# Cross-attention on one core: keys and values of each batch from 15 block products over three thirds of the keys in place of 18 products over two halves

## Chip, cores and metric

The kernel runs on one core of a Trainium2 chip. The metric is the device time of one execution in microseconds. Three executions of the kernel before gave a median of 989.63 us (988.45 to 991.03). A further execution was profiled; it took 991.36 us, and the span that its profile covers, from the first to the last instruction, is 989.6 us. All numbers are fp32.

## What is computed

There are 16 batches. Each has 100 query rows of 640 numbers (x) and 722 context rows of 384, of which 718 are keys and values of an ordinary attention with 8 heads of 80, and the last 4 are tokens of a second, small attention. The result is projected, and the input is added. Cut to what matters:

```python
enc, ca = ctx[:, :718], ctx[:, 718:]
query, keyt, valt = x @ Wq, enc @ Wk, enc @ Wv
hs = mha(query, keyt, valt)                    # 8 heads, softmax over 718 keys
ca_q1 = einsum('btc,th->bch', ca, Wq_ca)[:, indices, :]
ca_hs1 = mha(ca_q1, x, x)                      # 100 rows, keys and values are x
ca_hs2 = mha(ca_hs1 @ Wq, ca @ Wk_ca, ca @ Wv_ca)   # 4 keys
out = (hs + ca_hs2) @ Wout + b_out + x
```

For this case three products matter most: keyt and valt (718 x 384 by 384 x 640 for each batch), and what they feed, the scores and the weighted sum of the values.

## The kernel before

The engines are TensorE (PE, matmuls into PSUM), VectorE (DVE) and ScalarE (ACT), which read PSUM, GpSimd (POOL), which works in SBUF alone, and SyncE (SP), from whose queue most DMAs are issued. [...]

The kernel runs over the batches b in one unrolled loop. A turn of the loop makes the scores of batch b, then its values and the keys of batch b + 1, then the weighted sum of batch b. In more detail:

- *Scores* (`scores`, matmuls at L507). s_ps = K^T Q for 718 keys in three pairs of blocks; ACT copies them to SBUF (st, L517). DVE takes the maximum over keys (L1022, L1041), and the class `Maximum` turns it over the partitions in steps: turned (transpose), quad, side and mx (reductions), spread (ACT copies), over (a transpose on DVE, L581). Then DVE subtracts `over` from st (L1007, three instructions of 1,600 columns), and ACT takes the exponential of each (L1017).
- *Values and keys* (`Blocks`, matmuls at L304). The keys are cut into two halves of 359, the first 256 of the 384 input columns into two chunks, and the weights' columns into two halves. A fast 2 x 2 scheme makes the product of the first two chunks from 7 block products in place of 8, and the third chunk adds 4: 11 matmuls of one block of rows. Values have three blocks of rows (128, 128 and 103 keys of each half), each with `first_half` and `second_half` over four PSUM banks, 33 matmuls of 320 columns. Keys have the first four of their five row chunks in two such groups, and the fifth, `last_keys` (L448), is made from 6 plain matmuls: 28 matmuls of 359 columns. A product's bank is read at each step, by an ACT copy where a result block begins and by a DVE add to what is already there otherwise.
- *Sums of inputs.* The scheme needs sums of blocks of the context. `enc_sums` makes them on POOL, four instructions of 359 columns for each batch (L352), one batch ahead. Those of the weights are made once, in batch 0, on POOL (`weight_sums`, L365). In batch 0 the values and keys are plain products (`first_values`, L279, and `first_keys`), and of these values the last six matmul groups come inside the loop's first turn.
- *Weighted sum.* a_ps (L1147), 96 matmuls of 81 columns, the 81st being the sum of the weights.
- *The small attention* (class `Second`): y_ps (L613), the scores on POOL (`scores1`, L648 and L655, ten or so instructions of 800 columns), z_ps (L676), `values2` on POOL (L738 and L745), the load vb (L695). `keys(b)` multiplies m, which the start computes for all batches, by a mask into m2 on POOL.
- *Output.* Rows are collected to chunks of 128 over the batches; hst_ps and o_ps (L816) come in some batches only, and the queries of two batches (q_ps, L422) in every second one.

From batch 0 on, PE, DVE and POOL run in the order in which the code stands (`tc.manual_schedule`); ACT's order was left to a scheduler, with `issue_after` in some places. SP and the DMA queues are ordered by the scheduler as well. [...]

PSUM is cut into two pools of four banks, ps4 and ps1. The context of a batch (enc, with three more columns of 359 for the sums) has two buffers, so that batch b + 2 is loaded when batch b's values are done.

Of the kernel before, what the change touches and what calls it, by code (L numbers as in the profile page):

```python
# [8 lines left out]
F32 = mybir.dt.float32  # L9
# [9 lines left out]
P = 128  # L19
HC = H // P  # L20
CC = CAD // P
KH = SK // 2

KC = [(u + k, P) for u in (0, KH) for k in (0, P)] + [(u + 2 * P, KH - 2 * P) for u in (0, KH)]
NP = len(KC) // 2

PAIR = [(0, 0), (1, 0), (0, 1), (1, 1), (2, 0), (2, 1)]
PC = [KC[PAIR.index((i, 0))] for i in range(NP)]
# [59 lines left out]
S1, S2, S4 = range(3)  # L88
T1, T2, T4 = range(3)
# [3 lines left out]
def kernel(  # L93
# [28 lines left out]
    ps4 = ctx.enter_context(tc.tile_pool(name="ps4", bufs=4, space=PSUM))  # L122
    ps1 = ctx.enter_context(tc.tile_pool(name="ps1", bufs=4, space=PSUM))

    def psum4(name, n=4):
        return [
            ps4.tile([P, 512], F32, tag="ps4", name=f"{name}_{j}") for j in range(n)
        ]

    def four1(name):  # L130
        return [psum1(f"{name}_{j}") for j in range(4)]
# [3 lines left out]


    def wide(name):
        return main.tile([P, ROWS], F32, tag="wide", name=name, bufs=3)
# [7 lines left out]
    def hsT_tile(name):  # L146
        return main.tile([P, HC, P], F32, tag="hsT", name=name, bufs=3)

    def xn_tile(name):
        return main.tile([P, H], F32, tag="xn", name=name, bufs=3)  # L150
# [12 lines left out]
    def enc_tile(name):  # L163

        enc = inp.tile([P, CC * SK + 3 * KH], F32, tag="enc", name=name)
        return (
            enc[:, : CC * SK].rearrange("p (c k) -> p c k", c=CC),
            enc[:, CC * SK :].rearrange("p (j k) -> p j k", j=3),
        )

    def load_enc(b):
        enc = enc_tile(f"enc_{b}")
        nc.sync.dma_start(out=enc[0], in_=enct[b])
        return enc

# [3 lines left out]
    wv_sb = const.tile([P, CC, H], F32, name="wv_sb")  # L179
    wq_sb = const.tile([P, HC, H], F32, name="wq_sb")  # L180
    wk_sb = const.tile([P, CC, H], F32, name="wk_sb")
    kT = const.tile([P, HC, SK], F32, name="kT")
    wout_sb = const.tile([P, HC, H], F32, name="wout_sb")
    bias = const.tile([P, H], F32, name="bias")


    wv2 = const.tile([P, 3, H // 2], F32, name="wv2")
    wk2 = const.tile([P, 3, 2, P], F32, name="wk2")
    wk4 = const.tile([P, P], F32, name="wk4")

    wvca_sb = enc_tile("wvca")[0][:, :, :H]
    enc = enc_tile("enc_0")
    for c in range(CC):
        in_order(nc.sync.dma_start(out=enc[0][:, c, :P], in_=enct[0][:, c, :P]))
    for cols in slice(0, H // 2), slice(H // 2, H):
        for c in range(CC):
            nc.scalar.dma_start(
                out=wv_sb[:, c, cols], in_=wv[c * P : (c + 1) * P, cols]
            )
    for lo, hi in [(P, KH), (KH, SK)]:  # L200
        in_order(nc.sync.dma_start(out=enc[0][:, :, lo:hi], in_=enct[0][:, :, lo:hi]))
# [5 lines left out]
    wqt_sb = wout_sb  # L207
    in_order(nc.sync.dma_start(out=wqt_sb, in_=wqt.rearrange("(c p) r -> p c r", p=P)))
    xT = inp.tile([P, 2, HC, S], F32, tag="xT", name="xT_0")
    in_order(nc.sync.dma_start(out=xT, in_=xt[0:2].rearrange("b p c s -> p b c s")))  # L210
    for c in range(HC):
        in_order(nc.sync.dma_start(out=kT[:, c, :CAD], in_=packed(wkt, c)))  # L212
# [10 lines left out]
    vs = []  # L223
    for i in range(NP):
        v = const.tile([PC[i][1], 4, NH // 2, D + 1], F32, name=f"v_{i}")
        nc.gpsimd.memset(v[:, :, :, D : D + 1], 1.0)
        vs.append(v)

    def block(i, g):

        i, u = PAIR[i]
        return vs[i][:, 2 * u + g]
# [27 lines left out]
    m = const.tile([P, HC, B, HT], F32, name="m")  # L260
# [11 lines left out]
    def first_values(i, enc, engines, halves=(0, 1)):  # L272

        k, n = KC[i]
        for g in halves:
            engine = engines[g]
            v_ps = psum1(f"v_ps_0_{i}_{g}")
            for c in range(CC):
                nc.tensor.matmul(  # L279
                    v_ps[:n, : H // 2],  # L280
                    enc[0][:, c, k : k + n],
                    wv_sb[:, c, g * (H // 2) : (g + 1) * (H // 2)],
                    start=(c == 0),
                    stop=(c == CC - 1),
                )
            engine(
                block(i, g)[:, :, :D],
                v_ps[:n, : H // 2].rearrange("p (h d) -> p h d", d=D),
            )


    class Blocks:
        def __init__(self, name, a, w, to, view, swap):


            self.name, self.a, self.w, self.to, self.view = name, a, w, to, view
            self.swap = swap

        def sum(self, j, *products, first=False, last=False):
            bank = self.banks[j]  # L300
            for i, (a, w) in enumerate(products):
                a, w = self.a[a], self.w[w]
                left, right = (w, a) if self.swap else (a, w)
                nc.tensor.matmul(  # L304
                    bank[: left.shape[1], : right.shape[1]],
                    left,
                    right,
                    start=(first and i == 0),
                    stop=(last and i == len(products) - 1),
                    skip_group_check=True,  # L310
                )
            return self.view(bank)

        def first_half(self, room=None):

            self.banks = room or four1(f"{self.name}_ps")
            c11, c12, c21, c22 = self.to
            m = self.sum(0, ("11", "11"), first=True)
            self.copies = [nc.scalar.copy(c22, m)]
            m = self.sum(1, ("S2", "T2"), first=True)  # L320
            nc.vector.tensor_tensor(c21, m, c22, ALU.add)  # L321
            m = self.sum(2, ("S1", "T1"), first=True)
            nc.vector.tensor_tensor(c22, m, c22, ALU.add)
            m = self.sum(3, ("S3", "T3"), first=True)
            nc.vector.tensor_tensor(c22, m, c22, ALU.add)

        def second_half(self, behind=None, ahead=None):

            if ahead:
                ahead()  # L330
                behind = behind()
            c11, c12, c21, c22 = self.to
            m = self.sum(0, ("12", "21"), ("31", "31"), last=True)
            with tc.issue_after(behind.ins) if behind else nullcontext():
                self.copies.append(nc.scalar.copy(c11, m))
            m = self.sum(1, ("32", "32"), last=True)
            nc.vector.tensor_tensor(c22, m, c22, ALU.add)
            m = self.sum(2, ("S4", "22"), ("31", "32"), last=True)
            nc.vector.tensor_tensor(c12, m, c21, ALU.add)
            m = self.sum(3, ("22", "T4"), ("32", "31"), last=True)  # L340
            nc.vector.tensor_tensor(c21, m, c21, ALU.add)

    def sums(to, raw):

        (a11, a12), (a21, a22) = raw
        for out, left, right, op in (
            (to[S1], a21, a22, ALU.add),
            (to[S2], to[S1], a11, ALU.subtract),
            (a21, a11, a21, ALU.subtract),
            (to[S4], a12, to[S2], ALU.subtract),  # L350
# [3 lines left out]
    def weight_sums(to, raw, steps=range(4)):  # L354

        (w11, w12), (w21, w22) = raw
        all_steps = (
            (to[T1], w12, w11, ALU.subtract),
            (to[T2], w22, to[T1], ALU.subtract),
            (to[T4], w21, to[T2], ALU.subtract),  # L360
            (w12, w22, w12, ALU.subtract),
        )
        for i in steps:
            out, left, right, op = all_steps[i]
            nc.gpsimd.tensor_tensor(out, left, right, op)  # L365

    def enc_sums(enc):
        raw, to = enc
        sums(
            [to[:, j] for j in range(3)],  # L370
            [[raw[:, c, u * KH : (u + 1) * KH] for c in range(2)] for u in range(2)],
        )

    def a_blocks(enc, k, n):
        raw, to = enc
        half = lambda c, u: raw[:, c, u * KH + k : u * KH + k + n]
        blocks = {j: to[:, i, k : k + n] for j, i in (("S1", S1), ("S2", S2), ("S4", S4))}
        blocks |= {"11": half(0, 0), "12": half(1, 0), "S3": half(0, 1), "22": half(1, 1)}
        return blocks | {"31": half(2, 0), "32": half(2, 1)}

    def w_blocks(raw, to):
        blocks = {"T1": to(T1), "T2": to(T2), "T3": raw(0, 1), "T4": to(T4)}
        return blocks | {
            f"{c + 1}{u + 1}": raw(c, u) for c in range(CC) for u in range(2)
        }

    wv_blocks = w_blocks(
        lambda c, u: wv_sb[:, c, u * (H // 2) : (u + 1) * (H // 2)],
        lambda j: wv2[:, j],
    )  # L390
    wk_blocks = [
        w_blocks(
# [833 lines left out]
```

## Time and profile before

Busy time of the engines in some stretches of the profiled execution, in microseconds. The loop's turn for a batch begins with its scores.

| stretch | length | PE | DVE | ACT | POOL |
|---|---|---|---|---|---|
| whole span | 989.6 | 978.3 | 666.2 | 313.5 | 487.0 |
| first keys and queries, 43.1 to 61.2 | 18.10 | 18.10 | 6.92 | 4.02 | 9.55 |
| batch 0, 61.2 to 104.3 | 43.10 | 41.58 | 33.06 | 17.54 | 33.57 |
| batch 1, 104.3 to 165.4 | 61.10 | 59.85 | 43.23 | 21.03 | 34.37 |
| batch 2, 165.4 to 222.1 | 56.70 | 56.70 | 41.60 | 18.36 | 29.85 |
| batch 3, 222.1 to 287.0 | 64.90 | 64.90 | 41.60 | 20.20 | 29.86 |

How to read the rows of the profile: a row of the timeline has start, busy time, engine, line, operation, what it writes and reads (by the program's names; out<-in), sizes, and how many instructions were put together (xN). A bracket at the end has the idle time of the engine before the row and what ended it. A row of the groups has the busy time of all instructions of one kind and the mean of one in nanoseconds, then the idle time before them. Names are those of buffers, so a bank that was first used as `room` keeps that name. The chain of waits follows the work that ended last back through what released it.

### The profile page before, as it was taken

How to read it: one execution, taken by the hardware profiler on the slowest of the kernel's cores; microseconds unless marked ns; L12 is line 12 of the kernel's file. 1: busy time of each engine (PE TensorE's matmuls, PEld its weight loads, DVE VectorE, ACT ScalarE, POOL GpSimd, SP SyncE). 2: the span in 40 equal slices, each digit the busy share in tenths (PEclk: the TensorE clock that was granted, in tenths of full speed). 3: DMA queues.
4: the chain of work that ended last, by engine and by line, in shares of the span. 5: the costliest groups of instructions: out<-in, count | busy, mean ns of one | idle time of the engine just before them, and what ended most of it. 6: DMA issues, size and time to landing. Idle time of an engine off the chain costs nothing.

```text
span 989.6 us, 25057 instructions
## 1 busy us (share of the span) xinstructions
PE 978.3 (99%) x10945; PEld 746.6 (75%) x10945; DVE 666.2 (67%) x1227; ACT 313.5 (32%) x600; POOL 487.0 (49%) x440
## 2 busy tenths in 40 slices
PE   9999999999999999999999999999999999999998
PEld 6686869677696777868678686786868768697776
DVE  1249893967739677486955769468674776838784
ACT  1234342414333143332422333133331423314241
POOL 4557762665605646172652726536372562714604
PEclk9999999999999999999999999999999999999999
DMA  8642111120302202011120111201111030210101
GB/s 280 195 142 72 44 51 44 42 100 8 113 3 67 75 8 87 24 57 66 52 69 24 65 58 52 69 23 58 38 64 57 8 107 3 68 48 1 44 2 34
DMA packets 18533, 59.93 MB, mean 61 GB/s; under 512 B 2232, under 2 KB 9208, under 8 KB 14904
## 3 DMA queue, kind: packets, MB, share of 16 engines
q1 hardware_dynamic: 14888, 40.46, 12.5%
q0 software_dynamic: 2512, 16.72, 5.4%
q8 instruction: 86, 1.41, 0.6%
q10 hardware_dynamic: 1024, 1.15, 0.4%
q14 instruction: 23, 0.19, 0.1%
HBM read 54.07 MB, written 4.26 MB: 59 GB/s over the span
## 4 chain that ended last, share of the span: by engine, by line
PE 95%; DMA 2%; SPq 1%; DVE 1%; issue 1%; ACT 0%; ACTq 0%; DVEq 0%
PE room L304 19%; PE v_ps L304 18%; PE s_ps L507 12%; PE a_ps L1147 11%; PE k_ps L304 10%; PE kT_ps L448 7%; PE q_ps L422 7%; PE o_ps L816 6%; PE y_ps L613 2%; DMA wq<-in_wq 1%; SPq L212 1%; PE z_ps L676 1%; PE hst_ps L789 1%; PE v_ps L279 1%; DMA wv_sb<-in_wv 0%
## 5 line engine op out<-in xcount | busy, mean ns | idle before, releaser
L648 POOL TENSOR_TENSOR e<-ca,g 100x800 f32<-100x800 f32 x64 | 99.2, 1561 | 320.3 <-PE v_ps L304 248.6
L738 POOL TENSOR_TENSOR hs<-vb,p 100x640 f32<-100x640 f32 x64 | 83.9, 1322 | 135.9 <-DVE st L1007 105.0
L304 PE MATMUL v_ps<-wv_sb,enc 128*128 128x320 f32 (+1 forms) x480 | 149.5, 434 | 0.6 <-DVE v L321 0.6
L517 ACT COPY st<-s_ps 128x400 f32<-128x400 f32 (+1 forms) x192 | 80.6, 505 | 125.2 <-PE s_ps L507 125.1
L304 PEld LDWEIGHTS v_ps<-wv_sb,enc 128*128 128x128 f32 (+1 forms) x480 | 84.7, 179 | 42.4 <-DVE v L321 1.1
L1147 PEld LDWEIGHTS a_ps<-v,st 128*64 128x64 f32 (+3 forms) x3072 | 109.0, 125 | 7.6 <-issue 7.5
L1147 PE MATMUL a_ps<-v,st 128*64 128x81 f32 (+3 forms) x3072 | 112.0, 233 | 1.2 <-issue 1.2
L1017 ACT ACTIVATE st<-st 128x1600 f32<-128x1600 f32 (+1 forms) x48 | 73.8, 1538 | 101.8 <-DVE st L1007 101.8
L1007 DVE TENSOR_TENSOR st<-st,over 128x1600 f32<-128x1600 f32 (+1 forms) x48 | 104.1, 2174 | 0.0
L507 PE MATMUL s_ps<-qp,kT 32*128 32x100 f32 (+1 forms) x3072 | 99.6, 265 | 1.2 <-issue 1.2
L507 PEld LDWEIGHTS s_ps<-qp,kT 32*128 32x128 f32 (+1 forms) x3072 | 96.4, 181 | 3.1 <-issue 1.7
L655 POOL TENSOR_TENSOR e<-e,e 100x800 f32<-100x800 f32 x48 | 90.3, 1882 | 3.8
L304 PE MATMUL room<-enc,wk_sb 128*128 128x359 f32 x240 | 82.3, 465 | 0.0
L304 PE MATMUL k_ps<-enc,wk_sb 128*128 128x359 f32 x240 | 82.2, 464 | 0.0
L1022 DVE TENSOR_TENSOR most<-most,st 128x800 f32<-128x800 f32 (+1 forms) x64 | 65.1, 1016 | 25.3 <-ACT st L517 24.2
L745 POOL TENSOR_TENSOR hs<-hs,hs 100x640 f32<-100x640 f32 x48 | 74.0, 1541 | 3.8
L304 PE MATMUL room<-wv_sb,enc 128*128 128x320 f32 x240 | 74.4, 432 | 0.0
L422 PEld LDWEIGHTS q_ps<-xT,wq_sb 128*128 128x128 f32 x400 | 67.9, 190 | 2.1 <-issue 0.5
L448 PE MATMUL kT_ps<-enc,wk_sb 128*128 128x359 f32 x210 | 68.5, 465 | 0.8 <-DVE wk_sb L920 0.8
L422 PE MATMUL q_ps<-xT,wq_sb 128*128 128x200 f32 x400 | 69.1, 333 | 0.0
L1158 DVE RECIPROCAL rs<-a_ps 100x4 f32<-100x4 f32 x32 | 5.8, 181 | 92.8 <-PE a_ps L1147 92.7
L816 PE MATMUL o_ps<-wout_sb,hsT 128*128 128x320 f32 x240 | 66.8, 433 | 0.0
(138 smaller groups left out, 1535.5 us busy)
## 6 DMA issues: line engine op xcount, KB each, us to landing
enc<-in_enct SPq DMA_DIRECT2D x15, 1077.0 KB
vb<-va_d POOLq DMA_DIRECT2D x16, 1000.0 KB, 6.5
xT<-in_xt SPq DMA_DIRECT2D x8, 500.0 KB
xn<-in_x SPq DMA_DIRECT2D x12, 320.0 KB
out<-xn SPq DMA_DIRECT2D x11, 320.0 KB
ca<-in_cas SPq DMA_DIRECT2D x16, 156.2 KB
wout_sb<-in_wqt SPq DMA_DIRECT2D x1, 1600.0 KB
wq<-in_wq SPq DMA_DIRECT2D x5, 320.0 KB
```

The costliest lines, as they stand in the source:

```text
L304: nc.tensor.matmul(bank[: left.shape[1], : right.shape[1]], left, right, start=(first and i == 0), stop=(last and i == len(products) - 1), ...
L422: nc.tensor.matmul(q_ps[:, : 2 * S].rearrange("p (j s) -> p j s", j=2), wq_sb[:, c, n * P : (n + 1) * P], xT[:, :, c, :], start=(c == 0), ...
L448: nc.tensor.matmul(k_ps[:, :KH], w, a, start=(c == 0), stop=(c == CC - 1))
L507: nc.tensor.matmul(s_ps[r][:n, 256 * a + lo : 256 * a + hi], kT[rows, c, k : k + n], rhs, start=(a == 0 and c == 0), stop=(c == HC - 1), s ...
L517: copied = nc.scalar.copy(st[:, :, 2 * r * S : 2 * (r + 1) * S], s_ps[r][:n].rearrange("p (a q) -> p a q", a=2)[:, :, : 2 * S],)
L648: first = nc.gpsimd.tensor_tensor(to, self.ca[:, t, :].unsqueeze(1).to_broadcast([S, NH, S]), g[:, :, t].unsqueeze(2).to_broadcast([S, NH, ...
L655: nc.gpsimd.tensor_tensor(e, e, to, ALU.add)
L738: first = nc.gpsimd.tensor_tensor(to, vb[:S, t, :].rearrange("p (h d) -> p h d", h=NH), p2[:, :, t].unsqueeze(2).to_broadcast([S, NH, D]), ...
L745: nc.gpsimd.tensor_tensor(sums, sums, to, ALU.add)
L816: nc.tensor.matmul(o_ps[k][:n, : H // 2], hsTs[r][:, c, :n], wout_sb[:, c, k * (H // 2) : (k + 1) * (H // 2)], start=(c == 0), stop=(c == ...
L1007: less = nc.vector.tensor_tensor(st[i], st[i], top.over[:n].unsqueeze(1).to_broadcast([n, 2, ROWS]), ALU.subtract,)
L1147: nc.tensor.matmul(a_v[lo:hi, h % 4], st[i // 2][:, i % 2, h * S + lo : h * S + hi], block(i, h // 4)[:, h % 4], start=(i == 0), stop=(i = ...
```

## The change

The keys are cut into three thirds of 240, each overlapping the next by one key (KT = 240; a third u begins at key 239 u), and the 384 input columns into three chunks. A 3 x 3 by 3 x 2 scheme makes the six result blocks (third u, half g of the weights' columns) from 15 block products in place of 18. Two tables give its order: `V_PLAN` for values, `K_PLAN` for keys, each entry a bank, a product number and the result block that the bank is read into. Products go on adding up in the same bank after it was read.

- `Values` does two matmuls of 120 x 320 for each product (two halves of the third), `Keys` two of 128 x 240 (two chunks of the keys' rows). The fifth chunk of the keys stays plain: nine matmuls of 240 columns. For a batch that is 30 matmuls of 320 columns for values (33 before), and 39 of 240 for keys (28 of 359 before).
- A bank's reading (`Blocks.go`) is an ACT copy where the result block begins, and a DVE add otherwise. Banks A and B of the values are pairs of banks, read by one instruction of 640 columns. A read of the keys has 480 columns.
- PSUM is cut anew: ps2 has two pairs, psk two banks (A and B of the keys), ps1 two banks, for C, D and E of both values and keys and for y_ps, z_ps and a_ps.
- Products of the values of batch b and of the keys of batch b + 1 take turns (`both`), and `top.go` stands between them.
- `enc_sums` has 13 instructions of 240 columns. Two of the nine raw blocks of a batch lie in a tile of their own, `rest`, with one buffer, loaded by `load_rest`; the sums overwrite others. `weight_sums` has 12 steps, for wk on DVE, for wv on POOL (seven early, five late).
- m goes to DRAM (m_d, five writes from ACT's queue), and each batch loads its part (mb) from SP's queue.
- ACT too runs in the order of the code. The exponentials stand directly behind their subtractions, the third one behind the copies of `last_keys`.
- The tile `most` is kept, wide tiles have two buffers for three, and so have hsT and xn. Copies of the scores are two of 800 columns for two of the three pairs. The last batch uses free room of enc.

The diff, cut to its core. The first `open` is that of `Values`, which opens A and B beforehand, as pairs; the second is that of `Keys`. The orders at the end are those of batch 0 (it begins at `second.scores1()`) and of batches 1 to 14 (`second.scores1(seen)`):

```diff
-    ps4 = ctx.enter_context(tc.tile_pool(name="ps4", bufs=4, space=PSUM))
-    ps1 = ctx.enter_context(tc.tile_pool(name="ps1", bufs=4, space=PSUM))
+    ps2 = ctx.enter_context(tc.tile_pool(name="ps2", bufs=2, space=PSUM))
+    psk = ctx.enter_context(tc.tile_pool(name="psk", bufs=2, space=PSUM))
+    ps1 = ctx.enter_context(tc.tile_pool(name="ps1", bufs=2, space=PSUM))
...
+V_PLAN = [
+    ("A", 7, (2, 1)),
+    ("B", 13, (1, 0)),
+    ("D", 1, (2, 0)),
+    ("A", 3, (2, 0)),
+    ("B", 8, (2, 0)),
+    ("E", 6, (1, 0)),
+    ("A", 9, (1, 0)),
+    ("B", 10, (2, 1)),
+    ("C", 12, (0, 1)),
+    ("A", 2, (0, 0)),
+    ("C", 11, (2, 1)),
+    ("B", 4, (0, 1)),
+    ("A", 0, (0, 1)),
+    ("B", 14, (0, 0)),
+    ("A", 5, (1, 1)),
+]
+K_PLAN = [V_PLAN[k] for k in (0, 1, 2, 3, 4, 5, 6, 7, 9, 11, 8, 12, 10, 13, 14)]
...
+    def rest_tile(name):
+        return main.tile([P, len(A_REST), KT], F32, tag="rest", name=name)
...
+    def load_rest(b, enc):
+        rest = rest_tile(f"rest_{b}")
+        for (u, c), i in A_REST.items():
+            nc.sync.dma_start(
+                out=rest[:, i], in_=enct[b][:, c, u * (KT - 1) : u * (KT - 1) + KT]
+            )
+        return enc[0], rest
...
+        def go(self, n=1):
+            for _, (k, (bank, f, to)) in zip(range(n), self.plan):
+                first = bank not in self.opened
+                if first:
+                    self.opened[bank] = self.open(bank)
+                at = self.opened[bank]
+                self.product(at, f, first, self.ends[bank] == k)
+                for out, left in self.places(at, to):
+                    if to in self.begun:
+                        self.moved = nc.vector.tensor_tensor(out, left, out, ALU.add)
+                    else:
+                        self.moved = nc.scalar.copy(out, left)
+                self.begun.add(to)
...
+        def open(self, bank):
+            return [psum1(f"v_ps{bank}_{self.b}_{j}") for j in range(2)], None
...
+        def open(self, bank):
+            return (psumk if bank in "AB" else psum1)(f"k_ps{bank}_{self.b}")
...
+        nc.scalar.dma_start(out=m_d[c], in_=m_sb[c])
...
+            second.scores1()
+            weight_sums(nc.gpsimd, wv_sb, True)
+            top.go(3)
+            kk.go(3)
...
+            second.scores1(seen)
+            last.load()
+            top.go(3)
+            both(2)
+            both(1)
+            now.scores2()
+            top.go(1)
+            both(2)
+            top.go()
+            both(1)
+            both(2)
+            now.softmax3()
+            now.values2()
+            vv.go(2)
+            kk.go(1)
+            subtract(0)
+            exponential(0)
+            vv.go(2)
+            kk.go(2)
+            vv.go(1)
+            kk.go(2)
+            both(1)
+            both(1)
+            second.load()
+            second_next, enc_next, m_next = loads()
+            subtract(1)
+            exponential(1)
+            last_keys(b + 1, enc)
+            subtract(2)
+            exponential(2)
+            second.softmax1()
+            second.exponentials1()
+            last.project()
...
         if b + 2 < B:
-            keys(b + 2)
+            enc_next = load_rest(b + 2, enc_next)
+            keys(m_next)
             enc_sums(enc_next)
```

## Prediction

> **What bounds the kernel now.** I read the page's busy table and its chain first: PE is busy 978.3 of 989.6 us, and the chain that ended last is PE's to 95%.
>
> ```profile
> span 989.6 us, 25057 instructions
> PE 978.3 (99%) x10945; PEld 746.6 (75%) x10945; DVE 666.2 (67%) x1227; ACT 313.5 (32%) x600; POOL 487.0 (49%) x440
> ...
> PE 95%; DMA 2%; SPq 1%; DVE 1%; issue 1%; ACT 0%; ACTq 0%; DVEq 0%
> ```
>
> So a product taken away is worth its interval on PE, and a microsecond for which PE waits is paid in full. The intervals come from PE's timeline in batch 4, from one start to the next (the printed means of 430 to 465 ns are latencies that overlap). Each fp32 matmul stands in the records as two passes (10,945 records for the 5,520 matmuls of the program, a few records missing).
>
> ```profile
> 300.87 2.85 PE L304 MATMUL v_ps<-wv_sb,enc 128*128 128x320 f32 x10
> 303.56 0.70 PE L304 MATMUL v_ps<-wv,enc 128*128 128x320 f32 x2
> ...
> 333.38 3.18 PE L304 MATMUL k_ps<-enc,wk_sb 128*128 128x359 f32 x10
> 336.39 0.77 PE L304 MATMUL k_ps<-enc,wk 128*128 128x359 f32 x2
> ...
> 388.71 8.62 PE L422 MATMUL q_ps<-xT,wq_sb 128*128 128x200 f32 x50
> 397.25 6.97 PE L1147 MATMUL a_ps<-v,st 128*64 128x81 f32 x192
> ```
>
> 320 columns take 2.69/10 = 0.269 us a pass, 359 take 3.01/10 = 0.301, 200 take 8.54/50 = 0.171.
>
> The same view shows what a bank that is read late costs. The second V half of block c waits for DVE, which is in a long subtract; this is the one such stall in the batch:
>
> ```profile
> 311.47 2.89 DVE L1007 TENSOR_TENSOR st<-st,over 128x1600 f32<-128x1600 f32 x1
> 314.29 0.48 DVE L321 TENSOR_TENSOR v<-v_ps,v 103x320 f32<-103x320 f32 x1
> ...
> 314.81 1.92 PE L304 MATMUL v_ps<-wv_sb,enc 128*103 128x320 f32 x6 [0.60 <-DVE v L321]
> ```
>
> A DVE add on a K bank starts about 0.2 us after its product's interval ends: its idle of 0.68 is counted in this row from the end of the add before.
>
> ```profile
> 336.59 0.53 DVE L339 TENSOR_TENSOR kT<-k_ps,kT 128x359 f32<-128x359 f32 x1 [0.68 <-PE k_ps L304]
> ```
>
> In batch 0 the timelines of POOL and PE show that POOL makes batch 1's sums long before PE wants them:
>
> ```profile
> 60.41 3.53 POOL L352 TENSOR_TENSOR enc<-enc 128x359 f32<-128x359 f32 x4
> 63.89 0.74 POOL L365 TENSOR_TENSOR wk<-wk_sb 128x256 f32<-128x256 f32 x1
> 68.04 0.86 POOL L365 TENSOR_TENSOR wv<-wv_sb 128x320 f32<-128x320 f32 x1
> ...
> 73.96 6.65 PE L279 MATMUL v_ps<-wv_sb,enc 128*128 128x320 f32 x24
> 80.44 0.77 PE L304 MATMUL room<-enc,wk_sb 128*128 128x359 f32 x2
> ```
>
> **What the skill says.** "TensorE: Matmul & The Clock Gate", Back-to-back issue gap: N columns take about N/2.4 ns plus a fixed 2.5. Twice that for 320, 359 and 200 columns would be 272, 304 and 172 ns, against my 269, 301 and 171 for one record, so a pass here costs about 0.83 ns a column; 240 columns come to 0.2025 us a pass, 0.405 a matmul (an estimate, between the measured 200 and 320). "PSUM — Partial Sum Buffer", PSUM bank collisions raise a hardware error: PSUM is to be guarded by bank, so PE may not write a bank that is being read; and its section Engine vs sequencer instructions: the queues of VectorE and ScalarE are strictly first in, first out. The stall at 314.81 shows both. The clock gate's page, What's actually happening, has half clock after an idle window; the trace shows it once, 3.41 us at 0.5 from 68.9 us after a PE gap of 1.5 us, and not after gaps of 1.2 us.
>
> **The change part by part.**
>
> PE work. V goes from 33 matmuls of 320 columns to 30 in each of 15 batches: 3 x 2 x 0.269 = 1.61, x 15 = -24.2. K goes from 28 of 359 to 39 of 240: 28 x 2 x 0.302 = 16.91 against 39 x 0.405 = 15.80, x 15 = -16.7. The first keys, 30 of 359 to 45 of 240, +0.1. Scores (six blocks of 128 and 103 keys, now of 119 or 120) and the a_ps products keep count and columns: nothing. Sum -40.8.
>
> Bank waits in batches 1 to 14. Banks A and B of V are pairs, those of K have a pool of their own, but C, D and E of both take turns in two banks (ps1): vD0, vD1, kD, vE0, vE1, kE. So kE needs the bank of vE0 read, and only vE1 lies between. After the product kB, PE does vE0 and vE1, 2 x 0.54 = 1.08. DVE has after the same moment: 0.20 start, the add of kB (480 columns; 0.66, from 0.48 at 320 and 0.53 at 359 upwards), the transpose `over`, which the code puts ahead of vE0 in the queue, and vE0's add, 0.49, and 0.05 back to PE.
>
> ```profile
> L581 DVE STREAM_TRANSPOSE over<-spread 128x800 f32<-128x800 f32 x32 | 32.2, 1007 | 0.5
> ```
>
> 0.20 + 0.66 + 1.01 + 0.49 + 0.05 = 2.41, less 1.08 = 1.3 us, x 14 = +18.6. Bounds: 0.3 if `over` is already done, about 2.3 if DVE comes late. kD waits for ACT's copy of vD0, 0.20 + 0.44 + 0.05 - 0.54 = 0.15 to 0.19: +2.5. Other steps have a product or more in between, and the adds (V: 5,760 columns as before, in 11 instructions for 18) stay within PE's time.
>
> Start, first part. m goes to DRAM in five writes from ACT's queue; ACT's copy of y and with it the banks of w_ps stand behind them. The fourth write has to wait for the queue slot of a weight load: DVE's timeline has the copy of wq's fourth part (L928) start at 34.31, after 0.19 us <-DMA wq, so I put the w_ps chain, 29.0 to 31.7 now, 3.2 us later: +3.2 (0 to 5).
>
> Start, second part. The tile `rest` has one buffer. rest_1 may be loaded only when PE's last first_values of batch 0 has read rest_0: 80.4 us in the trace before, where enc_sums ran at 60.4. On SP it stands behind part of enc_2. From there POOL is one queue: landing 3.7 (estimate; out's 320 KB land within 2.2), 13 sums of 240 columns at 0.70 = 9.1 (estimate below wk's 0.74 at 256 and in the line of 0.94 at 359), seven wv sums at 0.86 = 6.0, scores1 12.1 (four products of 1.5, three adds of 1.9, one slowed), five late wv sums 4.3, values2 10.1, vb's issue 0.6, m2 1.4; then rest_2, which on SP stands behind the load of m for batch 4, which itself waits for that m2: 4.8; and seven sums until form 7 exists, 4.9. Together 57.0 (52 with sums at 0.63 by columns alone and landings of 2.2, 61 with 0.74 and landings of 6).
>
> ```profile
> L352 POOL TENSOR_TENSOR enc<-enc 128x359 f32<-128x359 f32 x60 | 55.1, 940 | 1.2
> ```
>
> PE in that time has K 15 x 0.81 = 12.15, last_keys 3.65, a_ps 6.9, scores 7.1, z, y and hst 2.65, two V products 2.15: 34.6, and then the first K product for batch 2 wants form 7. It loses 57.0 - 34.6 = 22.4 in all, 8 to 9 of it before its first K product in batch 0 (landing, and the first sums), the rest before K in batch 1. A stall of 1.25 us in this stretch of before goes: -1.25. A cold window of 3.41 us at half clock after such a gap: +1.7. Later batches are not held: POOL has 12.1 + 10.1 + 9.1 + 2 = 33 us in 55 to 64.
>
> Smaller ones. exp(2) is now behind the copies of last_keys on ACT, whose banks PE has only just written: 0.2 + 0.58 + 0.37 + 1.54 = 2.7 to a_ps, less what else PE has; only batches 10 and 14 have neither queries nor o_ps there, 2.2 each: +4.4. q_ps's last bank behind ACT in batches 1 and 5, 1.5 each: +3. The last batch, with exponentials now behind V's copies: +3. Stalls of before that go with its order (the 0.60 above, some others): -2.5. At nothing: m's load per batch, which lands half a batch before POOL's m2 (about 2.2 us on POOL if not); two wide, hsT and xn buffers for three, whose earlier user is done some 10 us before (a few us on DVE if not); and wk's 12 sums, now on DVE, about 5 us in batch 0 beside the scores, where DVE is busy for 33.1 of the 43.1 us from 61.2 to 104.3 (stage table) and PE stands later anyway.
>
> Sum: -40.8 + 21.1 + 3.2 + 22.4 - 1.25 + 1.7 + 4.4 + 3 + 3 - 2.5 = +14.3. The profiled execution has a span of 989.6 and took 991.4 us; the median of the runs is 989.63, so I add to 989.6: 1004 us. An even batch in the middle then takes about 55.3 us (now 56.5), an odd one 63.7 (64.9).
>
> **Rivals.**
> Bank waits are worse, or the clock falls: gaps of 1.3 us sit close to the 1.5 that set it to half once. Against it: gaps of 1.17 and 1.25 did not. For eight cold windows of 1.7 us, or a kE wait of 2.3 in place of 1.3 (DVE slowed by POOL, as its subtract is, 1.81 to 2.89), +14: 1018.
> The other side: the start costs nothing. Place: rest_1's load and POOL's chain behind it. If PE's wait there is for the first keys and not for the values (read out by 51 us), the sums are ready as before and all but the 3.2 goes: 1004 - 23 = 981. It decides for faster once this stretch costs under about 5 us in place of 23. For it: nothing else reads rest_0 in between. Against it: first_values(5) does read block (2,2), and a tile is released by its last reader.
> No change: kE's wait falls to 0.3, 14 less: 990. For it: only if ACT's spread is ready earlier, so that `over` ends before kB's add.
>
> **How the numbers follow.** My forecast has 0.57 (own range 994 to 1015), the slow rival 0.19, the fast one 0.17, no change 0.07. About 0.3%, 3 us, is what a measurement of this kernel can tell. Half of the no-change case falls to slower or faster: faster 0.20, same 0.05, slower 0.75. 982 to 1022 leaves out the worst of the slow rival and the fast one's better half.
>
> **What would show it.** kE's matmul at L447 with idle of about 1.3 <-DVE v in each of batches 1 to 14; a PE gap of 7 to 9 us at about 84 us and one of 12 to 14 us in batch 1, both <-POOL enc; middle batches shorter by about 1.2 us; PE busy near 937. I am wrong if POOL's sums for batch 1 run before 80 us, if kE stands without a wait, or if 240 columns cost more than 0.21 us a pass.

## The result and the profile after

The changed kernel takes 1014.0 us (median of 4 runs, 1011.9 to 1016.53), beside 990.33 us of the kernel before on the same chip: a ratio of 1.0242, interval 1.0213 to 1.0271, some 24 us slower. The forecast was 1004 us, its range 982 to 1022. Its profiled execution took 1016.53 us and has a span of 1014.8 us; that of the kernel before 989.6.

The page of the changed kernel, its span, its busy times and the shares of the chain that ended last:

```profile
span 1014.8 us, 25610 instructions
...
PE 957.9 (94%) x11215; PEld 806.1 (79%) x11215; DVE 667.9 (66%) x1078; ACT 360.4 (36%) x596; POOL 627.0 (62%) x577
...
PE 72%; DVE 15%; POOL 5%; ACT 3%; DMA 2%; SPq 2%; issue 1%; ACTq 0%; DVEq 0%; POOLq 0%
```

PE is busy for 20 us less, and yet the span is 25 us longer: PE now waits. Where it does so is seen from the stages. The rows are batches 0 to 3 of the changed kernel (from the first score to the next batch's first score); columns are the length, the busy time of PE, PEld (loads of weights into PE), DVE, ACT and POOL, each with the number of instructions, then the granted TensorE clock as a share of full speed, the DMA share and GB/s.

```profile
69.80:125.60 55.80, 43.83 (x612) 38.19 (x612) 31.04 (x54) 18.80 (x30) 34.93 (x33) 0.88 0.15 44
125.60:200.30 74.70, 63.95 (x701) 53.97 (x699) 44.22 (x70) 23.80 (x40) 60.45 (x59) 0.91 0.17 51
200.30:255.60 55.30, 54.31 (x675) 45.23 (x671) 41.77 (x66) 21.44 (x34) 32.89 (x27) 1.00 0.22 66
255.60:319.30 63.70, 62.71 (x721) 53.71 (x719) 42.06 (x66) 23.38 (x40) 43.90 (x42) 1.00 0.16 49
```

Batch 2 takes 55.3 us, batch 3 63.7: each 1.2 to 1.4 us shorter than before (56.7 and 64.9). Batches 0 and 1 take 55.8 and 74.7 in place of 43.1 and 61.1, and batch 0 begins at 69.8 in place of 61.2. At the start of batch 2 the changed kernel is 34.8 us behind (200.32 against 165.48); it then makes up 13.5 us until batch 14, and loses 3.9 in the last two. So what the change wins, it wins batch by batch, and what it loses, it loses mostly before 200 us.

PE's timeline of the changed kernel shows the long waits of that start, each with what ended it in the bracket:

```profile
38.33 1.54 PE L1027 MATMUL w_ps<-ident,kT 128*128 128x128 f32 x6 [5.22 <-ACT y L739]
...
94.71 1.97 PE L447 MATMUL k_psA<-enc,wk_sb 128*128 128x240 f32 x4 [9.19 <-POOL enc L482]
...
138.51 0.65 PE L718 MATMUL y_ps<-m,xT 128*100 128x96 f32 x2 [3.09 <-POOL m L693]
...
149.43 1.97 PE L447 MATMUL k_psA<-enc,wk_sb 128*128 128x240 f32 x4 [3.30 <-POOL enc L482]
```

The first belongs to m's writes. ACT's timeline: five writes are issued from 29.71 on, the queue is held for 8.16 us, and only then can y be copied.

```profile
29.71 8.16 ACTq L1016 DMA_DIRECT2D m_d<-m  x5
37.91 0.37 ACT L739 COPY y<-y_ps 100x256 f32<-100x256 f32 x1 [20.06 <-DMA m_d<-m]
```

The others belong to POOL. Its timeline after the last first_values (by the intervals of the products PE ends them at 85.36):

```profile
89.73 0.69 POOL L482 TENSOR_TENSOR enc<-enc,rest 128x240 f32<-128x240 f32 x1 [22.16 <-DMA rest<-in_enct]
...
98.88 5.79 POOL L503 TENSOR_TENSOR wv_sb<-wv_sb 128x320 f32<-128x320 f32 x7
...
136.91 4.25 POOL L693 TENSOR_TENSOR m<-mb,hmask 128x64 f32<-128x64 f32 x5
144.42 0.69 POOL L482 TENSOR_TENSOR enc<-enc,rest 128x240 f32<-128x240 f32 x1 [3.25 <-DMA rest<-in_enct]
```

POOL stood for 22.16 us until rest_1 landed, 4.4 us after first_values had read rest_0. From that read to the first key product for batch 2 (149.43) it took 64.1 us: the landing, and then one queue of POOL, with one more wait of 3.25 us for the landing of rest_2. PE's waits bring a cold clock with them: after the gap of 9.19 us the granted clock is 0.50 from 94.7 to 99.6, and the key products follow each other at 1.76 and 1.60 us in place of 0.81.

In the steady batches one wait of size is left, that of kE, the key product that opens bank E. PE and DVE in batch 2 of the changed kernel:

```profile
218.64 0.97 PE L447 MATMUL k_psB<-enc,wk_sb 128*128 128x240 f32 x4
219.45 1.24 PE L416 MATMUL v_psE<-wv_sb,enc 128*120 128x320 f32 x4
221.68 1.08 PE L447 MATMUL k_psE<-enc,wk_sb 128*128 128x240 f32 x4 [0.99 <-DVE vs L387]
```

```profile
219.67 0.66 DVE L387 TENSOR_TENSOR kT<-k_psB,kT 128x480 f32<-128x480 f32 x1
220.25 1.00 DVE L677 STREAM_TRANSPOSE over<-spread 128x800 f32<-128x800 f32 x1
221.17 0.85 DVE L387 TENSOR_TENSOR vs<-v_psE,vs 120x320 f32<-120x320 f32 x2
```

vE's two matmuls take 1.08 us, but 2.23 pass between the starts of vE and kE: 1.15 us of wait (0.99 in the bracket, because the modelled ends of the products lie behind their intervals). DVE's row order is the reason at a glance: kB's read, `over`, and only then the two reads of vE, the first of which frees kE's bank.

### The profile page after: what moved, and what is told of

It is laid out like the page before. It is cut to its first block, busy times and chain, and to the rows that moved or that the text cites. A ratio compares the mean times of both kernels' runs of the same rounds, so it can differ in the third digit from the quotient of the medians.

```text
span 1014.8 us, 25610 instructions
## 1 busy us (share of the span) xinstructions
PE 957.9 (94%) x11215; PEld 806.1 (79%) x11215; DVE 667.9 (66%) x1078; ACT 360.4 (36%) x596; POOL 627.0 (62%) x577
## 4 chain that ended last, share of the span: by engine, by line
PE 72%; DVE 15%; POOL 5%; ACT 3%; DMA 2%; SPq 2%; issue 1%; ACTq 0%; DVEq 0%; POOLq 0%
PE a_ps L1260 10%; PE s_ps L595 9%; PE v_psA L416 8%; PE v_psB L416 6%; PE o_ps L923 6%; PE kT_ps L540 6%; PE q_ps L516 5%; PE k_psA L447 5%; PE k_psB L447 4%; PE v_psC L416 3%; DVE most L1121 3%; PE k_psC L447 2%; DVE kT L387 2%; DVE over L677 2%; DVE vs L387 2%; PE k_psE L447 1%
## 5 line engine op out<-in xcount | busy, mean ns | idle before, releaser
L1260 PEld LDWEIGHTS a_ps<-vs,st 120*64 120x64 f32 (+3 forms) x3072 | 112.4, 127 | 11.4 <-ACT st L1117 6.5
L1260 PE MATMUL a_ps<-vs,st 120*64 120x81 f32 (+3 forms) x3072 | 115.5, 237 | 5.7 <-ACT st L1117 5.7
L416 PE MATMUL v_psA<-wv_sb,enc 128*120 128x320 f32 x360 | 113.2, 437 | 1.5 <-DVE vs L387 1.5
L1109 DVE TENSOR_TENSOR st<-st,over 120x1600 f32<-120x1600 f32 x48 | 104.6, 2206 | 0.0
L482 POOL TENSOR_TENSOR enc<-enc,rest 128x240 f32<-128x240 f32 x45 | 34.5, 766 | 112.7 <-DMA rest<-in_enct 112.7
L447 PE MATMUL k_psA<-enc,wk_sb 128*128 128x240 f32 x360 | 90.1, 374 | 13.1 <-POOL enc L482 12.5
L482 POOL TENSOR_TENSOR enc<-enc 128x240 f32<-128x240 f32 x135 | 97.5, 736 | 7.1
L595 PE MATMUL s_ps<-qp,kT 32*120 32x100 f32 x3072 | 98.3, 263 | 1.4 <-DVE hs L1273 1.4
L595 PEld LDWEIGHTS s_ps<-qp,kT 32*120 32x120 f32 x3072 | 95.4, 179 | 3.2 <-issue 1.8
L447 PEld LDWEIGHTS k_psA<-enc,wk_sb 128*128 128x128 f32 x360 | 69.6, 194 | 30.9 <-POOL enc L482 13.5
L416 PE MATMUL v_psB<-wv_sb,enc 128*120 128x320 f32 x300 | 93.1, 433 | 0.0
L447 PE MATMUL k_psB<-enc,wk_sb 128*128 128x240 f32 x300 | 74.7, 372 | 0.0
```

What stands on the lines that cost most here:

```text
L416: nc.tensor.matmul(at[0][j][:KN, : H // 2], a_form(self.enc, f)[:, j * KN : (j + 1) * KN], wv_sb[:, W_AT[f]], start=first, stop=last, skip ...
L447: nc.tensor.matmul(at[:, i * KT : (i + 1) * KT], wk_sb[:, W_AT[f], i], a_form(self.enc, f), start=(first and i == 0), stop=last, skip_grou ...
L595: nc.tensor.matmul(s_ps[r][:n, 256 * a + lo : 256 * a + hi], kT[rows, c, u, j * KN : (j + 1) * KN], rhs, start=(a == 0 and c == 0), stop=( ...
L1109: return nc.vector.tensor_tensor(st[i], st[i], top.over[:KN].unsqueeze(1).to_broadcast([KN, 2, ROWS]), ALU.subtract,)
L1260: nc.tensor.matmul(a_v[lo:hi, h % 4], st[i // 2][: KEYS[i], i % 2, h * S + lo : h * S + hi], block(i, h // 4)[: KEYS[i], h % 4], start=(i ...
```

## Experiments

All are edits of the changed kernel unless told otherwise. Behind each time stands its ratio to the kernel before on the same chip, with the interval of that ratio.

### Two buffers for rest

```diff
-        return main.tile([P, len(A_REST), KT], F32, tag="rest", name=name)
+        return main.tile([P, len(A_REST), KT], F32, tag="rest", name=name, bufs=2)
...
-    idle = small.tile([P, P], F32, tag="idle", name="idle")
+    idle = qpool.tile([P, 1, 2, 2 * S], F32, tag="qz", name="idle")[:, 0, 0, :P]
```

> Changed kernel with two buffers for the tile rest, so that rest_1 need not wait for the last first_values (the start's scratch tile moves into qz to make room). Theory (the start is lost to rest_1's load and the POOL chain behind it): the 9.2 us gap before the first K product of batch 0 goes, and so do the waits on POOL in batch 1; scores of batch 2 start near 174 us in place of 200, about 988 us in all. Rival (POOL's larger work at the start, 13 sums of 240 columns and 12 of 320, holds PE by itself): only some 12 us come back, about 1002 us, and PE still waits for POOL enc L482 in batch 1.

Measured: 1001.71 us, ratio 1.0119 (1.0103 to 1.0136). The gap of 9.2 us is gone, batch 0 takes 44.9 us and batch 1 67.3, but the scores of batch 2 start at 186.6, and PE still waits for POOL in batch 1 (2.8 us at y_ps and 1.8 at k_psA). The second change of the diff only makes room: the start's scratch tile moves into another. The time is the rival's, and so is the wait in batch 1. One part of it is neither's: in PE's timeline the wait at w_ps has grown from 5.2 to 10.2 us.

```profile
43.61 1.54 PE L1027 MATMUL w_ps<-ident,kT 128*128 128x128 f32 x6 [10.23 <-ACT y L739]
```

ACT's five writes of m were held for 12.7 us in place of 8.2. The chain of waits leads from the last write back to the load of wvca, in the changed kernel to that of wq; the new loads of rest_1 are issued at that time (36.8 to 39.3 us), but that it is they that hold the write is inferred. So the edit gave back 18.3 us in batches 0 and 1 and took 4.6 before them. Of the 26 us by which these two batches are longer than in the kernel before, the one buffer accounts for 18, the cold clock behind its waits included.

### over behind the products E

```diff
             both(2)
-            top.go()
             both(1)
+            top.go()
             both(2)
```

> Changed kernel with top.go() (the transpose over) behind the products E of values and keys in place of ahead of them. Theory (kE waits because over stands ahead of vE0's add on DVE): the wait of kE falls from 1.15 to 0.15-0.35 us in each of batches 1 to 14, 11 to 14 us less, about 1001 us. Rival (DVE is short of time there whatever the order): the wait turns up at kE or at the next A, B or C bank again, within 4 us of 1014.

Measured: 1001.79 us, 1.0119 (1.0104 to 1.0134). PE and DVE in batch 2 of this run:

```profile
219.06 1.24 PE L416 MATMUL v_psE<-wv_sb,enc 128*120 128x320 f32 x4
220.39 1.08 PE L447 MATMUL k_psE<-enc,wk_sb 128*128 128x240 f32 x4
```

```profile
219.85 0.97 DVE L387 TENSOR_TENSOR vs<-v_psE,vs 120x320 f32<-120x320 f32 x2
221.51 0.66 DVE L387 TENSOR_TENSOR kT<-k_psE,kT 128x480 f32<-128x480 f32 x1 [0.68 <-PE k_psE L447]
222.08 1.00 DVE L677 STREAM_TRANSPOSE over<-spread 128x800 f32<-128x800 f32 x1
```

1.33 us pass from vE to kE, a wait of 0.25 in place of 1.15, and a middle batch takes 54.4 or 62.8 us, 0.9 less. The place of one instruction in DVE's order cost 12 us of the kernel, and nothing of it came back elsewhere.

### m's writes behind w_ps

```diff
-        nc.scalar.dma_start(out=m_d[c], in_=m_sb[c])
...
+    with tc.issue_after(split.ins):
+        for c in range(HC):
+            nc.scalar.dma_start(out=m_d[c], in_=m_sb[c])
```

(`split` is the last copy out of w_ps.)

> Changed kernel with the five writes of m to DRAM behind the copies of w_ps on ACT's queue. Theory (y's copy behind the writes holds the w_ps banks): the gap of 5.2 us at 33 us goes and the cold clock after it, 5 to 7 us less, about 1008 us. Rival (the loads that land then, wq and wkt, set the end anyway): under 2 us gained.

Measured: 1011.44 us, 1.0208 (1.0188 to 1.0228), 2.6 us less, between the two. The gap of 5.2 us goes and batch 0 begins at 66.1 in place of 69.8. But the kernel before began at 61.2; what then ends last is a load, seen in PE's timeline of this run:

```profile
32.67 2.34 PE L1026 MATMUL w_ps<-ident,kT 128*128 128x128 f32 x9 [1.93 <-DMA kT<-in_wkt]
```

### The third exponential first

```diff
-            last_keys(b + 1, enc)
             subtract(2)
             exponential(2)
+            last_keys(b + 1, enc)
```

> Changed kernel with subtract(2) and exponential(2) in the program ahead of last_keys, in all batches; PE's order stays. Theory (a_ps waits for an exponential that stands behind last_keys' copies on ACT): the waits of a_ps in batches 0, 10 and 14 (2.1, 1.6 and 1.9 us) go, 3.5 to 6 us less, about 1009.5 us. Rival (the subtraction on DVE ends too late itself): under 1.5 us gained.

Measured: 1014.17 us, 1.0245 (1.023 to 1.026): nothing. DVE and ACT of this run in batch 14:

```profile
944.67 5.86 DVE L1109 TENSOR_TENSOR st<-st,over 120x1600 f32<-120x1600 f32 x2
```

```profile
950.62 1.54 ACT L1117 ACTIVATE st<-st 120x1600 f32<-120x1600 f32 x1 [1.55 <-DVE st L1109]
952.06 0.80 ACT L551 COPY kT<-kT_ps 128x480 f32<-128x480 f32 x2
```

The exponential does stand ahead of the copies now, and still begins at 950.62, because the second subtraction of this row (the third of the batch) ends then; a_ps waits 1.9 us as before, and 2.1 in batch 0 as before. Only batch 10 gained (a wait of 0.6 in place of 1.6). In the whole the rival holds: but for that 1.0 us, DVE's subtractions, 2.9 us each here, set it, not ACT's order.

### The three edits together

The edits of rest, over and m's writes.

> The edits of the two rest buffers, of over behind the products E, and of m's writes behind the w_ps copies together. Theory (the three losses are separate in place and add up; with m's writes out of the way the start no longer moves later): scores of batch 2 start near 178 us (12 to 13 us later than in the kernel before), middle batches of 54.4 and 62.8 us, about 978 us. Rival (they cover each other, POOL's chain in batch 0 and 1 holds PE all the same): 984 us or more, scores of batch 2 after 184 us.

Measured: 982.18 us, 0.9933 (0.9921 to 0.9945): 0.7% faster than the kernel before, and 31.8 us less than the changed kernel, where the three alone add up to 27.1. The three alone and the three together ran on different chips, and by the spans of the profiles it is 34.5 against 33.9, so the three do not cover each other, and that they gain more together is not shown. What is shown is that with m's writes behind w_ps the second buffer no longer makes the start later: batch 0 begins at 66.8, beside 66.1 with the writes moved alone and 74.4 with the buffer alone. Scores of batch 2 start at 180.2, between the two expectations: batch 1 still takes 68.4 us, 3.2 of it in waits for POOL.

### The early sums of wv ahead of those of the context

```diff
-            enc_sums(enc)
             weight_sums(nc.gpsimd, wv_sb, False)
+            enc_sums(enc)
```

> The same, and the seven early sums of wv ahead of the 13 sums of the context in POOL's order, where POOL waits for the load of enc_1 anyway. Theory (what is left in batches 0 and 1 is POOL's chain from enc_1's landing to m2 and form 7 for batch 2): the waits of y_ps (3.2 us) and k_psA (1.8 us) on POOL in batch 1 shrink to under 1 us together, 4 us less than the kernel without this edit, about 974 us. Rival (DVE's subtractions and reductions set batches 0 and 1): within 1.5 us of it.

Measured: 981.52 us, 0.9923 (0.9912 to 0.9935), where the theory expected 974: 0.7 us less than without the edit, and the two intervals overlap. The waits on POOL in batch 1 are gone and it takes 61.7 us, 6.7 less, more than the theory's 4; but batch 0 takes 50.2 in place of 45.0. PE waits for DVE there, and DVE's and POOL's timelines say why:

```profile
82.38 4.58 PE L357 MATMUL v_ps<-wv_sb,enc 128*120 128x320 f32 x10 [4.46 <-DVE z L791]
```

```profile
64.64 7.29 DVE L770 TENSOR_TENSOR e<-e,over 100x800 f32<-100x800 f32 x1
```

```profile
64.67 5.76 POOL L503 TENSOR_TENSOR wv_sb<-wv_sb 128x320 f32<-128x320 f32 x7
```

One subtraction of 800 columns, 1.6 us in the run before, stood for 7.3 us, until POOL's seven sums, which need not wait for each other, and the first sum of the context had gone by. The gain in batch 1 was paid with a wait that no bracket shows.

### The same sums where POOL has nothing to do

The same edit, but the call stands at the head of batch 0, ahead of `now.load()`. POOL then comes to the sums at 12.83 us.

> The three edits, and the seven early sums of wv at the head of batch 0 in the code, ahead of vb's load, where POOL comes to them near 10 to 20 us and DVE is not in an instruction with two SBUF inputs. Theory (in the run before, DVE's e - over stood still for 7.3 us because POOL's seven sums ran beside it): e - over takes under 2 us again, z_ps and first_values wait for nothing on DVE, batch 0 takes about 45 us and batch 1 about 62, near 975.5 us. Rival (PE would wait in batch 0 anyway, for POOL's sums or the maxima): batch 0 at 48 us or more, 979 or more.

Measured: 976.43 us, 0.9869 (0.9851 to 0.9888), the best of all: 13 us less than the kernel before, 38 less than the changed one. Batch 0 takes 42.7 us and batch 1 62.5. DVE and POOL of this run:

```profile
63.95 1.59 DVE L770 TENSOR_TENSOR e<-e,over 100x800 f32<-100x800 f32 x1
```

```profile
12.83 5.77 POOL L503 TENSOR_TENSOR wv_sb<-wv_sb 128x320 f32<-128x320 f32 x7
```

The subtraction is back at 1.6 us, one sum of POOL beside it (0.99 us in the changed kernel, where POOL stood). Against the run before, nothing in its own queue or its inputs was changed, only what POOL does beside it. So the seven sums are shown to be the cause.

### The sums of wk behind the maxima

The kernel of the last run, with `weight_sums(nc.vector, wk_sb, late)` moved behind `seen = larger(2)`.

> The same, and the twelve sums of wk on DVE behind the maxima of batch 0, so that they no longer lie beside POOL's 13 sums of the context. Theory (the two sets hold each other): POOL's 13 sums take 9 to 11 us in place of 16 to 17, the waits on POOL in batch 1 end, up to 2 us less than without this edit. Rival (POOL's sums are slow by themselves in this stretch): they still take over 15 us.

Measured: 987.57 us, 0.998 (0.9972 to 0.9988), 11 us more than without the edit. The theory's first half holds: POOL's 13 sums take 11.3 us (66.25 to 77.5) in place of 17. Its second half does not: DVE's twelve sums now lie beside scores1 and the late sums of wv on POOL, and take 16.45 us in place of 5.4.

```profile
82.20 16.45 DVE L503 TENSOR_TENSOR wk_sb<-wk_sb 128x256 f32<-128x256 f32 x12
```

```profile
100.27 1.94 PE L447 MATMUL k_psA<-enc,wk_sb 128*128 128x240 f32 x4 [15.87 <-ACT vs L364]
```

```profile
99.62 0.23 ACT L819 ACTIVATE e<-e 100x32 f32<-100x32 f32 x1 [20.09 <-DVE e L816]
99.76 1.39 ACT L364 COPY vs<-v_ps 120x320 f32<-120x320 f32 x4
```

PE's wait of 15.87 us ends with the first of these ACT copies, which frees the bank of a first_values product. The copy had not been held by PE: it stood in ACT's queue behind the exponential of the small attention, which waited 20.09 us for DVE's e, and that e stood in DVE's queue behind the twelve sums of wk (the last ends at 98.65). So the twelve sums set the wait, through two queues. Batch 0 takes 59.3 us in place of 42.7; batch 1 has no wait on POOL any more and takes 58.9 in place of 62.5. The contention is not removed by moving the sums, only exchanged.

## Why the prediction was right, and where it was too low

Direction and mechanism came out as put: slower, from the start and from one bank wait. Against the forecast span of 1003.9 us the profile has 10.9 more: 5.4 ahead of batch 0, some 4 in batches 0 and 1, 1.6 in batch 14. Step by step:

*PE work.* Forecast 2.7 us less a batch, with bank waits of 1.5 put against it, so 55.3 and 63.7 us for a middle even and odd batch. Measured 55.3 and 63.7; 240 columns cost 0.2025 us a pass as estimated (four in 0.81). (For a pass of 359 columns the sum took 0.302 us where the prediction had read 0.301; that is 0.8 us in all.) For batches 2 to 13 the terms of the sum come to -13.5 us, and the traces give -13.5. So close an agreement is in part luck: batch 11 waited 1.1 us longer at kE than the others, and q_ps and a_ps together 0.8 less than put.

*Bank waits.* Forecast 1.3 us at kE, measured 1.15, and moving `over` alone takes it to 0.25. The cause is shown, not only the size. In batch 11 alone the wait was 2.25 us, the slow rival's size: DVE came late, after a small subtraction (L816) that took 1.18 us there and 0.19 in batch 1.

*Start, first part: mis-sized.* m's writes were put at 3.2 us; batch 0 begins 8.6 us later than before. The mechanism was as put, for the chain of waits leads from the last write to a load of wq, but it held ACT for 8.2 us, and the first key products after the gap took 1.4 us longer at half clock. The range of 0 to 5 did not hold it. The third experiment shows that moving the writes takes 3.7 us of the 8.6 away. In the rest the load of wkt has 1.9 us, and the first key products still run at half clock; it was not taken apart further.

*Start, second part: mis-sized.* The chain from first_values to form 7 for batch 2 was put at 57.0 us and took 64.1. Landing (4.4 against 3.7), the 13 sums (9.1 as put) and the seven sums of wv (5.8 against 6.0) were about right, values2 took 10.8 (10.1 put), and the wait for rest_2 was 3.3 in place of 4.8. scores1 took 16.6 in place of 12.1, for it lay beside DVE's subtractions, and m2 4.25 in place of 1.4, beside DVE's maxima. Both durations had been taken from rows in which POOL worked alone; batch 0 of the kernel before already had scores1 at 13.5 us (74.56 to 88.03). One cold window of 1.7 us was counted; from the intervals of the value and key products, the cold clock took 3.0 us in batch 0 and 4.0 in batch 1, of which only the 2.9 after 149.43 add to the chain. Against that, a gap of 1.5 us and its cold window in batch 0 of the kernel before went away, which the sum had left out.

*Signs.* The gap before the first key product of batch 0 came (9.2 us, 8 to 9 put). The one of 12 to 14 us in batch 1 did not: PE waits for POOL 3.8 us at y_ps, for m2, and 3.3 at the key product. The rest of the chain's time had gone by before, in half clock, in a wait of 2.1 us at a_ps in batch 0 with 1.5 us of cold clock behind it, which was not forecast, and in one of 1.4 us for DVE. PE was busy for 957.9 us, not near 937: products at half clock count as busy for as long as they take, and a middle even batch lost 2.2 us of busy time (56.49 to 54.27), not 2.7.

*Smaller ones.* q_ps waits 1.2 us in batches 1 and 5 (1.5 put). Batches 10 and 14 wait for the third exponential, 1.6 and 1.9 us (2.2 put), but for the most part not for the reason given: the fourth experiment takes the copies away from ahead of it, and of the waits only 1.0 us in batch 10 goes. In batch 14 a cold window of 1.6 us followed the wait, which the sum did not have. The last batch loses 1.3 us (1.4 from the sum).

The rival of the other side, a start that costs nothing, fell with rest_1's load: it leaves at 85.7 us, behind first_values. The slow rival was right in part: cold windows came at the start and in batch 14. Its longer wait at kE came in batch 11 only, and neither there nor behind the gaps of 1.15 us in the other steady batches did the clock leave 1.00. What it and the forecast both put too low is POOL slowed by DVE, some 7 us in scores1 and m2.

The middle batches show that the scheme of 15 products is a gain: with the three repairs it is 0.7% faster than the kernel before, and with the sums of wv made early 1.3%. What stays open: how much of the 18 us of the first experiment is POOL's chain and how much the clock was not taken apart; nor was it tried to take the contention of POOL's sums and DVE's sums away altogether.

## What to carry to other kernels

Where one engine sets the time, count a change in two parts, what it takes from that engine and which new releases it makes the engine wait for; then read for each release what stands ahead of it in the releasing engine's queue, since one transpose in the wrong place cost 12 us here. A tile with one buffer at the start is not a small matter: its load cannot leave before its last reader, and everything queued behind the first use on that engine moves along with it. And a duration from a row holds only beside the neighbours that it had there: before moving work between VectorE and GpSimd, see what the other one does at that time.

## What the runs showed of the hardware

VectorE and GpSimd hold each other where VectorE has two inputs in SBUF. The Trainium skill, "SBUF — State Buffer", Who interferes with whom, has it that such an instruction contends with a GpSimd instruction that reads SBUF. The runs agree and add sizes. A DVE subtraction of 800 columns took 1.0 us with GpSimd standing, 1.6 beside one of its sums and 7.3 beside eight; twelve DVE sums of 256 columns took 5.4 us or 16.45; GpSimd's 13 sums of 240 columns took 9.1 us alone and 17 beside those sums. Small ones suffer too: GpSimd's m2 products take 0.3 us in the kernel before, and in the changed one, where they come to lie beside DVE's subtractions or maxima, up to 1.97; all five together took 4.25 us in batch 1. This row shows their spread in the changed kernel (duration in ns, least, median and greatest):

```profile
L693 POOL TENSOR_TENSOR m<-mb,hmask x70: 283/344/1969, 136.9 to 887.7; 128x64 f32<-128x64 f32 x42, 128x96 f32<-128x96 f32 x28
```

Where both have a run of instructions that wait for nothing, which of them stands still went either way: in the run with the early sums of wv it was DVE, in the run without it POOL, whose second sum of the context took 4.36 us beside DVE's sums.

How long PE's gap was did not alone decide whether the clock fell. In batch 14, a_ps begins after a wait of 1.9 us in the changed kernel and in all eight experiments. In the profiles of the changed kernel, of m's writes moved and of the sums of wv made first, the granted clock behind that wait fell to half for most of the next 4 us (means of 0.50 to 0.74 over stretches of up to 2 us); in the other six it stayed at 1.00. The same 176 records took 8.04 us in the changed kernel and 6.41 with the three edits:

```profile
953.75 8.04 PE L1260 MATMUL a_ps<-vs,st 119*64 119x81 f32 x176 [1.94 <-ACT st L1117]
```

```profile
920.89 6.41 PE L1262 MATMUL a_ps<-vs,st 119*64 119x81 f32 x176 [1.93 <-ACT st L1119]
```

In the kernel before a gap of 1.52 us was followed by 0.50, and in the changed kernel gaps of 1.64 (batch 10) and 2.09 us (batch 11) were not.
